# A decoder on one core: LayerNorm statistics of the first two layers by summing passes of ScalarE, and the first group of the first layer placed in front of the tables

## The chip, the cores and the metric

The kernel runs on one core of a Trainium2 chip. The metric is the device time of one execution in microseconds (us), and of several runs the median. A core has five engines that work side by side, each on its own queue, in order: TensorE (PE in the profile; PEld is its weight load), VectorE (DVE), ScalarE (ACT), GpSimd (POOL) and SyncE (SP), which here only issues DMA transfers. An engine that needs another's result waits on a semaphore; everything queued behind the waiting instruction waits too.

## The reference

The input is x, 64 sequences of 128 rows by 256 columns in float32, with a context of the same shape and a mask. Six sublayers follow one another, each of the form x = x + f(layernorm(x)):

```python
def _layernorm(x, axis=-1, eps=1e-05):
    m = jnp.mean(x, axis=axis, keepdims=True)
    v = jnp.var(x, axis=axis, keepdims=True)
    return (x - m) / jnp.sqrt(v + eps)

# 1 window attention: each row attends to 7 neighbours, 16 heads of 16
scores = jnp.einsum('bhld,bhlwd->bhlw', Q, Kw) / sqrt(DH)
fw = softmax(scores) * conn                # conn: a small MLP of the offset
fw = fw / (fw.sum(axis=-1, keepdims=True) + 1e-09)
out = jnp.einsum('bhlw,bhlwd->bhld', fw, Vw) @ wo.T + bo
# 2 first cross attention: queries layernorm(x), keys and values ctx, masked
score = jnp.where(sm == 0, -1e9, q @ k / sqrt(DK))
out = ((softmax(score) * sm) @ v @ Wp.T + bp) * mask
# 3 a slot layer   4 self attention with a bias from distances
# 5 a second cross attention   6 an MLP with quantised values and a convolution
```

The connection table conn depends on weights alone: two layers with a Gelu, and a softmax over the 7 offsets.

## The kernel before, in words

The 64 sequences are worked in 16 groups of four (`GB = 4`). A group's x is one tile of 128 rows by 4 by 256, and eight such tiles are in use in turn. `Flow.reach` (L81) issues the load of a group's x on SP, and the store of finished groups; between the layers x goes through memory in the device. The code lists the operations in a loop order; a scheduler then gives each engine its own order from its estimates, so an engine's queue may differ from the order of the lines.

**Statistics.** There are two ways to get a group's mean and variance. `ln_stats` (L142 to L145) has VectorE make `bn_stats` and `bn_aggr` for each of the four sequences, adds epsilon, and has GpSimd raise the result to -0.5; `row_bias` (L290) then makes -mean × rs on VectorE. `act_means` (L153) and `act_deviations` (L164 to L172) use ScalarE: four Identity passes whose output is thrown away and whose sum is the negative mean, four Square passes with that mean as bias, then one VectorE product-and-sum (L169), the power on GpSimd (L170) and one VectorE product (L172). In the kernel before, the window layer and the first cross layer use the first way; a later layer uses the second.

**The start.** `setup` makes the unit matrix. `prep_window` loads the projection weights, then makes `gather` and `spread` (constant matrices which sum over, or copy to, the 16 columns of a head) and the connection table, in its own PSUM pool `psP`. Only then `stage_window` begins.

**The window layer** (`stage_window`) is a software pipeline over slots, one slot per sequence: `window_project` is a generator whose parts are called one by one, first statistics, then the scaled rows (L299, ScalarE) with the addition of bo into x (L314, GpSimd), transposes (L322, copies L325), and the projections (L194) of q and k per half, copied out by ScalarE (qt L331, pad L336), and of v (pad L341). In step with it run the products q × shifted k on GpSimd (L348, two per sequence), their sums per head on TensorE (L360), once per group the softmax over 7 offsets on VectorE (L376 to L389, exp on ScalarE L379), the spreading of its weights on TensorE (L400), the products with shifted v and their sums on VectorE (L406, L410), and the output projection (L203) whose result VectorE adds to x (L420). At the last slot of the first groups the preparation of the later layers is emitted (`later`): tables and weights for the first cross layer, the slots, the MLP, the self attention and its bias.

PSUM is split into `psA` with three tiles (projections, outputs), `s1A` with one (scores of a group), `scA` with two (spread weights).

**The first cross layer** (`stage_cross0`, about 555 to 1290 us together with the slots): `prep(bi)` is called for each sequence ahead of its attention. At the first sequence of a group it issues the loads of the next group, takes the statistics, scales them by 0.25 (L711) and makes the row bias; then ScalarE writes the normalised query (qp, L720), TensorE transposes it, ScalarE copies it out (qt, L737). Scores are made in two bursts of sixteen heads (L519, tiles sm and se), a maximum on VectorE (L546) and an exp on ScalarE (L542) follow. One tile set of scores exists at a time (`scB`, one buffer).

All SBUF pools wait tile by tile when a new pool takes the memory of an old one (`reuse_waits="tile"`); the PSUM pools wait for the whole old pool.

Of the kernel before, what the change touches and what calls it, by code (L numbers as in the profile page):

```python
# [10 lines left out]
F = mybir.dt.float32  # L11
BF = mybir.dt.bfloat16
AF = mybir.ActivationFunctionType
ALU = mybir.AluOpType
AX = mybir.AxisListType

D = 256
H = 16
DH = 16
S = 128  # L20
WIN = 7
SLOTS = 64
GB = 4
# [88 lines left out]
def load_row(k, pool, name, parts=128):  # L112
    ap = k.a[name]
    t = pool.tile([parts, ap.shape[0]], F, name="t_" + name)
    k.nc.gpsimd.dma_start(out=t, in_=ap.partition_broadcast(parts))
    return t


def psum(k):
    return k.ps.tile([128, 512], F, tag="ps", name="ps")  # L120
# [88 lines left out]
def prep_window(k, pool):  # L209
    nc, a = k.nc, k.a  # L210
    w = Ctx()
    w.wq = load(k, pool, "a_wq")
    w.wk = load(k, pool, "a_wk")
    w.wv = load(k, pool, "a_wv")
    w.wo = load(k, pool, "a_wo")
    w.bo = load_row(k, pool, "a_bo")

    w.gather = pool.tile([128, GB, GB, 8], F, name="gather")
    nc.gpsimd.memset(w.gather, 0.0)
    for b in range(GB):  # L220
        nc.vector.tensor_reduce(
            w.gather[:, b, b, :], k.ident.rearrange("p (h d) -> p h d", d=DH), AX.X, ALU.add
        )

    w.spread = pool.tile([128, GB, 128], F, name="spread")
    for b in range(GB):
        four = pool.tile([128, 4, GB * 8], F, name="four", tag="four", bufs=1)
        nc.vector.tensor_copy(
            four, w.gather[:, b].rearrange("p b h -> p (b h)").unsqueeze(1).to_broadcast([128, 4, GB * 8])
        )  # L230
        p = psum(k)
        nc.tensor.transpose(p[:, 0:128], four.rearrange("p q i -> p (q i)"), k.ident)
        nc.scalar.copy(w.spread[:, b, :], p[:, 0:128])
    w.conn = pool.tile([128, WIN], F, name="conn")
    n = WIN * H
    with k.tc.tile_pool(name="connw", bufs=1) as cp:
        cw1 = load(k, cp, "a_cw1")
        cb1 = load(k, cp, "a_cb1")
        cw2 = load(k, cp, "a_cw2")
        cb2 = load(k, cp, "a_cb2")  # L240
        cw3 = load(k, cp, "a_cw3")
        cb3 = load(k, cp, "a_cb3")
        pos = load(k, cp, "a_pos")
        h1 = cp.tile([n, 32], F, name="h1")
        nc.vector.scalar_tensor_tensor(h1, cw1, pos[:, 0:1], cb1, ALU.mult, ALU.add)
        nc.scalar.activation(h1, h1, AF.Gelu)
        pr = cp.tile([n, 32, 32], F, name="pr")
        nc.vector.tensor_tensor(
            pr, cw2.rearrange("p (j i) -> p j i", i=32),
            h1.unsqueeze(1).to_broadcast([n, 32, 32]), ALU.mult,  # L250
        )
        h2 = cp.tile([n, 32], F, name="h2")
        nc.vector.tensor_reduce(h2, pr, AX.X, ALU.add)
        nc.vector.tensor_tensor(h2, h2, cb2, ALU.add)
        nc.scalar.activation(h2, h2, AF.Gelu)
        nc.vector.tensor_tensor(h2, h2, cw3, ALU.mult)
        cw = cp.tile([n, 1], F, name="cw")
        nc.vector.tensor_reduce(cw, h2, AX.X, ALU.add)
        nc.vector.tensor_tensor(cw, cw, cb3, ALU.add)
        dg = cp.tile([128, n], F, name="dg")  # L260
        nc.gpsimd.memset(dg, 0.0)
        nc.vector.tensor_scalar(dg[:n], k.ident[:n, :n], cw[:, 0:1], None, ALU.mult)
        p = psum(k)
        nc.tensor.matmul(p[:, 0:n], k.ones, dg, start=True, stop=True)
        e = cp.tile([S, WIN, H], F, name="ce")
        pv = p[:, 0:n].rearrange("p (w h) -> p w h", h=H)
        m = cp.tile([S, H], F, name="cm")
        nc.vector.tensor_reduce(m, pv.rearrange("p w h -> p h w"), AX.X, ALU.max)
        nc.vector.tensor_tensor(e, pv, m.unsqueeze(1).to_broadcast([S, WIN, H]), ALU.subtract)
        nc.scalar.activation(e, e, AF.Exp)  # L270
        sm = cp.tile([S, H], F, name="csm")
        nc.vector.tensor_reduce(sm, e.rearrange("p w h -> p h w"), AX.X, ALU.add)
        nc.vector.reciprocal(sm, sm)
        nc.vector.tensor_tensor(
            e, e, sm.unsqueeze(1).to_broadcast([S, WIN, H]), ALU.mult,
        )

        mine = cp.tile([128, H], F, name="mine")
        iv = k.ident.rearrange("p (t c b h) -> p c h t b", t=2, c=2, b=GB)
        for c in range(2):  # L280
            nc.vector.tensor_reduce(mine[:, 8 * c : 8 * c + 8], iv[:, c], AX.XY, ALU.add)
        nc.vector.tensor_tensor(e, e, mine.unsqueeze(1).to_broadcast([S, WIN, H]), ALU.mult)
        nc.vector.tensor_reduce(w.conn, e, AX.X, ALU.add)
    return w


def row_bias(k, pool, mv, rs):
# [16 lines left out]
def window_project(k, w, g, wp, w1, kt, vt):  # L304

    nc = k.nc
    t = Ctx()
    t.g, t.kt, t.vt = g, kt, vt
    k.flow.reach(g + 1)
    mv, rs = ln_stats(k, wp, g)  # L310
    yield t
    xn = w1.tile([S, GB, D], F, tag="xn", name="xn")
    scaled_rows(k, wp, g, mv, rs, xn)
    nc.gpsimd.tensor_tensor(  # L314
        k.x[g], k.x[g], w.bo.unsqueeze(1).to_broadcast([S, GB, D]), ALU.add
    )
    yield t
    xnT = w1.tile([128, 2, GB * S], F, tag="xnT", name="xnT")
    for kc in range(2):
        p = psum(k)  # L320
        for b in range(GB):
            nc.tensor.transpose(  # L322
                p[:, b * S : (b + 1) * S], xn[:, b, kc * 128 : (kc + 1) * 128], k.ident
            )
        nc.scalar.copy(xnT[:, kc, :], p)  # L325
    yield t
    t.qt = wp.tile([128, 2, GB, S], F, tag="qt", name="qt")
    for c in range(2):
        p = psum(k)
        project(k, p, w.wq, c * 128, 128, xnT, 0, GB * S)  # L330
        nc.scalar.activation(  # L331
            t.qt[:, c], p.rearrange("p (b l) -> p b l", l=S), AF.Copy, scale=0.25
        )
        p = psum(k)
        project(k, p, w.wk, c * 128, 128, xnT, 0, GB * S)
        nc.scalar.copy(kt[:, c, :, 3 : 3 + S], p.rearrange("p (b l) -> p b l", l=S))  # L336
        yield t
    for c in range(2):
        p = psum(k)
        project(k, p, w.wv, c * 128, 128, xnT, 0, GB * S)  # L340
        nc.scalar.copy(vt[:, c, :, 3 : 3 + S], p.rearrange("p (b l) -> p b l", l=S))  # L341
    yield t
# [77 lines left out]
    k.nc.vector.tensor_tensor(xb, py[:, 0:D], xb, ALU.add)  # L420


def stage_window(k, w, later):


    nc = k.nc
    with k.tc.tile_pool(name="wa", bufs=2) as wp, k.tc.tile_pool(name="wa1", bufs=1) as w1:
# [8 lines left out]
        def project_part(g):  # L436
            if g in parts:
                groups[g] = next(parts[g], groups.get(g))

        for n in range(-3, GB * (k.G + 3) + 3):  # L440
# [6 lines left out]
            v, vb = divmod(n - 2 * GB - 2, GB)  # L447
            if 0 <= v < k.G:
                values[vb] = window_values(k, w, groups[v], vb, wp)
            if b in (1, 2):  # L450
                project_part(s + 1)
            if b == 0 and s - 2 in groups and s - 2 < k.G:
                window_softmax(k, w, groups[s - 2], wp, w1)
            c, cb = s - 1, b
# [232 lines left out]
def stage_cross0(k, w, slots):  # L687
# [3 lines left out]
    with k.pool("wb", 2) as wp, k.pool("wb1", 1) as w1, k.pool("wb3", 3) as w3:  # L691
# [8 lines left out]
        k.flow.reach(0)  # L700
        stats = {}

        def prep(bi):
            g, b = divmod(bi, GB)
            if b == 0:
                k.flow.reach(min(g + 1, k.G - 1))
                if g + 1 < k.G:
                    cxs[g + 1] = load_group(k, wp, g + 1, 3)
                mv, rs = ln_stats(k, early, g)
                r4 = early.tile([S, GB], F, tag="r4", name="r4")  # L710
                nc.vector.tensor_scalar(r4, rs, 0.25, None, ALU.mult)  # L711
                stats[g] = r4, row_bias(k, early, mv, r4)
            r4, nm = stats[g]
            mk = w.mask[:, bi : bi + 1]
            if b == GB - 1 and g + 1 < k.G:
# [882 lines left out]
def decoder(tc, a):  # L1598
# [8 lines left out]
    k.pool = pool  # L1607

    def scores(name, bufs):
        return tc.tile_pool(name=name, bufs=bufs, space=bass.MemoryType.PSUM)  # L1610

    with ExitStack() as ctx:
        k.res = ctx.enter_context(tc.tile_pool(name="res", bufs=1))
# [12 lines left out]
        w0 = right.enter_context(k.pool("w0", 1, "right"))  # L1626
        with tc.tile_pool(name="wB", bufs=1) as wB, tc.tile_pool(name="wbe", bufs=2) as wbe:
            with tc.tile_pool(name="wA", bufs=1) as wA:
                with scores("psP", 4) as k.ps:
                    wa = prep_window(k, wA)  # L1630

                def prep_b():
                    p.b = prep_cross0(k, wB, wbe)

                def prep_c():
                    p.c = prep_slots(k, w0)

                def prep_d():
                    p.d = prep_proj(k, w1, "d")

                fire = prep_fire(k, w1)

                def prep_bias():
                    next(fire)

                def prep_f():
                    p.f = prep_bitnet(k, k.res)

                with scores("psA", 3) as k.ps, scores("s1A", 1) as k.s1, \
                        scores("scA", 2) as k.sc:  # L1650
                    stage_window(k, wa, [prep_b, prep_c, prep_f, prep_d] + [prep_bias] * 6)
            k.ps = ctx.enter_context(scores("ps", 4))
            score = ExitStack()
            k.sc = score.enter_context(scores("scB", 1))
# [135 lines left out]
```

## Time and profile before

| what | value |
|---|---|
| runs | 3015.18, 3021.71, 3022.23 us; median 3021.71 |
| profiled execution | 3018.02 us, span 3016.2 us |
| mean granted TensorE clock | 0.947 |
| PE busy | 2744.6 us (91%) |
| DVE busy | 2272.4 us (75%) |
| ACT busy | 1676.4 us (56%) |
| POOL busy | 453.7 us (15%) |
| L142 bn_stats, whole kernel | 256 of 402 ns |
| L164 Square pass with sum, later layer | 64 of 493 ns |
| L153 Identity pass with sum, later layer | 64 of 413 ns |
| L348 product on GpSimd | 128 of 2014 ns |

In the profile a group of instructions is a row: line, engine, operation, output and inputs by the program's names, shapes, count, then busy time and mean duration, then the idle time of the engine just before them and what ended it. A row of waits names the engine and the tile that waited, what it waited for, the total in us, the number of times and the longest. A row of the chain is a start, a length and the piece of work that set the end.

The softmax of a window group begins with its maximum (L376). Over the 16 groups that starts at 63.4, 91.6, 127.6, 163.7, 212.9, 239.8, 265.7, 292.6, 331.8, 365.7, 392.7, 419.0, 452.1, 478.0, 503.3 and 527.7 us.

### The profile page before, as it was taken

The numbers are of one execution on the slowest core, as the hardware profiler recorded it, in microseconds if no ns is written. First come the engines' busy times: TensorE is split into PE (matmuls) and PEld (weight loads), VectorE is DVE, ScalarE is ACT, GpSimd is POOL, SyncE is SP. The second block draws the span as 40 slices with busy tenths as digits, with TensorE's granted clock in tenths as the row PEclk, the third lists the DMA queues.
The fourth block names the chain that finished last, engine by engine and source line by source line (L and its number), as shares of the span: only waits on it lengthen the run. The fifth ranks groups of instructions, "written<-read, shape, count | busy, mean of one in ns | idle before, by whom it ended". The sixth has DMA issues, their size and how long they took to land.

```text
span 3016.2 us, 63840 instructions
## 1 busy us (share of the span) xinstructions
PE 2744.6 (91%) x26972; PEld 1769.6 (59%) x26972; DVE 2272.4 (75%) x4341; ACT 1676.4 (56%) x2988; POOL 453.7 (15%) x356
## 2 busy tenths in 40 slices
PE   5789999888988889999999999999999998999998
PEld 2334533576666666666666667666666666444454
DVE  5888789757777777688899889854555545799987
ACT  3132221265666666665666666555556564777764
POOL 7566565000000000100000000110000000000000
PEclk9889899689999999999999999999999899999999
DMA  5101011211111110000200000111111101001100
GB/s 153 42 30 42 29 42 42 70 29 41 58 35 53 44 51 23 29 29 29 78 29 30 30 30 29 36 44 43 43 44 43 43 23 36 26 31 42 36 22 28
DMA packets 60012, 123.83 MB, mean 41 GB/s; under 512 B 9088, under 2 KB 34064, under 8 KB 59472
## 3 DMA queue, kind: packets, MB, share of 16 engines
q1 hardware_dynamic: 59168, 118.28, 11.5%
q8 instruction: 213, 3.49, 0.5%
q0 software_dynamic: 560, 1.49, 0.2%
q14 instruction: 71, 0.58, 0.1%
HBM read 77.76 MB, written 41.98 MB: 40 GB/s over the span
## 4 chain that ended last, share of the span: by engine, by line
PE 52%; DVE 29%; ACT 12%; POOL 3%; DMA 3%; issue 2%; SPq 0%; POOLq 0%; DVEq 0%; ACTq 0%
PE ps L194 9%; PE ps L203 9%; PE sm L519 8%; PE se L519 4%; PE ps L572 4%; PE cv L1442 4%; PE ps L1240 4%; DVE negmax L546 3%; DVE pv L406 2%; DVE sb L533 2%; ACT e L542 2%; DVE e L539 2%; DVE hs L1496 2%; DVE oT L410 2%; PE ps L584 2%
## 5 line engine op out<-in xcount | busy, mean ns | idle before, releaser
L519 PE MATMUL sm<-kt,qt 32*128 32x128 f32 x6144 | 538.3, 298 | 52.5 <-DVE negmax L546 31.2
L519 PEld LDWEIGHTS sm<-kt,qt 32*128 32x128 f32 x6144 | 436.7, 193 | 224.4 <-DVE negmax L546 69.1
L546 DVE TENSOR_REDUCE negmax<-sm 128x8 f32<-128x1024 f32 x256 | 312.3, 1220 | 291.3 <-PE se L519 252.2
L519 PE MATMUL se<-q,kt 32*128 32x128 f32 x6144 | 486.6, 292 | 43.2 <-ACT e L542 25.8
L519 PEld LDWEIGHTS se<-q,kt 32*128 32x128 f32 x6144 | 406.5, 193 | 70.9 <-ACT e L542 31.5
L542 ACT ACTIVATE e<-se 128x1024 f32<-128x1024 f32 x256 | 261.3, 1021 | 181.6 <-PE se L519 177.0
L348 POOL TENSOR_TENSOR pr<-pad,qt 128x896 f32<-128x896 f32 x128 | 254.8, 2014 | 137.0 <-PE s L360 97.7
L577 ACT COPY avs<-ps 128x512 f32<-128x512 f32 x192 | 112.0, 583 | 150.5 <-PE ps L572 150.5
L533 DVE TENSOR_TENSOR sb<-sm,bias_s 128x1024 f32<-128x1024 f32 x128 | 156.1, 1220 | 46.9 <-PE se L519 35.8
L145 POOL TENSOR_TENSOR ln_rs<-ln_ve,expo 128x4 f32<-128x4 f32 x64 | 66.2, 1036 | 734.6 <-DVE ln_ve L144 624.6
L540 ACT ACTIVATE e<-e 128x1024 f32<-128x1024 f32 x128 | 135.2, 1056 | 71.7 <-DVE e L539 70.9
L406 DVE TENSOR_TENSOR pv<-sc,pad 128x896 f32<-128x896 f32 x128 | 138.9, 1091 | 25.9 <-PE sc L400 25.8
L539 DVE TENSOR_TENSOR e<-se,bias_t 128x1024 f32<-128x1024 f32 x128 | 155.3, 1214 | 0.0
L546 DVE TENSOR_REDUCE negmax<-sb 128x8 f32<-128x1024 f32 x128 | 154.6, 1208 | 0.0
L572 PE MATMUL ps<-e,dva 128*32 128x128 f32 x4096 | 149.0, 289 | 2.7 <-ACT e L542 2.0
L410 DVE TENSOR_REDUCE oT<-pv 128x128 f32<-128x896 f32 x128 | 138.9, 1091 | 1.0
L572 PEld LDWEIGHTS ps<-e,dva 128*32 128x32 f32 x4096 | 111.4, 115 | 44.4 <-issue 30.5
L400 PE MATMUL sc<-fw,spread 32*128 32x448 f32 x512 | 106.5, 663 | 32.7 <-DVE pv L406 27.8
L560 DVE TENSOR_TENSOR q<-ps,qt 128x512 f32<-128x512 f32 x192 | 130.6, 680 | 1.7 <-PE ps L558 1.7
L584 PE MATMUL ps<-ident,avs 128*128 128x128 f32 x768 | 120.8, 282 | 0.1
L142 DVE BATCH_NORM_STATS2 ln_st<-x 128x6 f32<-128x256 f32 x256 | 98.1, 402 | 23.4 <-DMA x<-ef 14.7
L170 POOL TENSOR_TENSOR as_r<-as_s,expo 128x4 f32<-128x4 f32 x16 | 16.1, 1008 | 552.9 <-DVE as_s L169 552.9
(360 smaller groups left out, 5913.4 us busy)
## 6 DMA issues: line engine op xcount, KB each, us to landing
x<-in_x_dram SPq DMA_DIRECT2D x16, 512.0 KB
kt<-in_ctxT_dram SPq DMA_DIRECT2D x128, 64.0 KB
ab<-x SPq DMA_DIRECT2D x16, 512.0 KB
x<-ab SPq DMA_DIRECT2D x16, 512.0 KB
cx<-in_ctx_dram SPq DMA_DIRECT2D x16, 512.0 KB
cd<-x SPq DMA_DIRECT2D x16, 512.0 KB
x<-cd SPq DMA_DIRECT2D x16, 512.0 KB
de<-x SPq DMA_DIRECT2D x16, 512.0 KB
```

The costliest lines, as they stand in the source:

```text
L194: k.nc.tensor.matmul(out, w[:, kc, c0 : c0 + cn], rhsT[:, kc, n0 : n0 + n], start=(kc == 0), stop=(kc == 1),)
L203: k.nc.tensor.matmul(out, aT[:, kc, :], w[:, kc, :], start=(kc == 0), stop=(kc == 1))
L348: k.nc.gpsimd.tensor_tensor(pr[:, c], shift_windows(t.kt, b, c), t.qt[:, c, b, :].unsqueeze(1).to_broadcast([128, WIN, S]), ALU.mult,)
L406: nc.vector.tensor_tensor(pv, bc[th][:, :, 0 : WIN * 64].rearrange("p c (l w) -> p c l w", w=WIN), shift_windows2(t.vt, b, th), ALU.mult,)
L410: nc.vector.tensor_reduce(oT[:, :, 64 * th : 64 * th + 64], pv, AX.X, ALU.add)
L519: k.nc.tensor.matmul(ts[side][:, rr, c * S : (c + 1) * S], st[rows, c, :], mv[rows, c, :], start=True, stop=True,)
L533: nc.vector.tensor_tensor(sb, src, bias_s[:, hf * 2 : hf * 2 + 2, :], ALU.add)
L539: nc.vector.tensor_tensor(e, est, bias_t[:, hf * 2 : hf * 2 + 2, :], ALU.add)
L542: nc.scalar.activation(e, est, AF.Exp)
L546: nc.vector.tensor_reduce(b.lay.extra(b.nm, hf * 2), src.rearrange("p r (c m) -> p r c m", m=S), AX.X, ALU.max, negate=True,)
L572: nc.tensor.matmul(av[32 * r : 32 * r + 32, c * S : (c + 1) * S], b.va[:, b.lay.head(c, r), :], b.e[r // 2][:, r % 2, c * S : (c + 1) * S] ...
L584: nc.tensor.transpose(tv[:, c * S : (c + 1) * S], b.avs[:, c, :], k.ident)
```

## The change

Four parts.

1. In the window layer a group's statistics are taken by `act_means` and `act_deviations`, as two parts of the generator, and the tile `xn` of the normalised rows takes their thrown-away output. The generator of the next group is now advanced in three slots of four (`b >= 1`), where it was two.
2. `prep_window` only loads weights. `prep_spread` and `prep_connection` are called inside the slot loop, at n = 4 and n = 6, so that the first group's projection is emitted in front of them. `prep_spread` uses one PSUM tile and one copy for all four matrices, and borrows the tile `xnT`. The pool `psP` is gone.
3. PSUM pools, too, wait tile by tile.
4. In the first cross layer the statistics of group g + 1 are taken by passes of ScalarE during group g (at its third sequence), those of group 0 before the loop. The passes write to one junk tile. Both results are scaled by 0.25.

```diff
@@ prep_window: the tables become functions of their own
+    return w
+
+def prep_spread(k, w, pool, w1):
     w.gather = pool.tile([128, GB, GB, 8], F, name="gather")
...
+    xnT = w1.tile([128, 2, GB * S], F, tag="xnT", name="four")
+    four = xnT[:, 0].rearrange("p (b q i) -> p b q i", b=GB, q=4)
+    p = psum(k)
     for b in range(GB):
-        four = pool.tile([128, 4, GB * 8], F, name="four", tag="four", bufs=1)
         nc.vector.tensor_copy(
-            four, w.gather[:, b].rearrange(...).to_broadcast([128, 4, GB * 8])
-        )
-        p = psum(k)
-        nc.tensor.transpose(p[:, 0:128], four.rearrange("p q i -> p (q i)"), k.ident)
-        nc.scalar.copy(w.spread[:, b, :], p[:, 0:128])
+            four[:, b], w.gather[:, b].rearrange(...).to_broadcast([128, 4, GB * 8])
+        )
+        nc.tensor.transpose(
+            p[:, b * 128 : (b + 1) * 128], four[:, b].rearrange("p q i -> p (q i)"), k.ident
+        )
+    nc.scalar.copy(w.spread, p.rearrange("p (b i) -> p b i", b=GB))
+
+def prep_connection(k, w, pool):
     w.conn = pool.tile([128, WIN], F, name="conn")
@@ window_project
-    mv, rs = ln_stats(k, wp, g)
+    xn = w1.tile([S, GB, D], F, tag="xn", name="xn")
+    means = act_means(k, wp, g, xn)
     yield t
-    xn = w1.tile([S, GB, D], F, tag="xn", name="xn")
-    scaled_rows(k, wp, g, mv, rs, xn)
+    rs, add = act_deviations(k, wp, g, xn, means)
+    yield t
+    scaled_rows(k, wp, g, None, rs, xn, add)
@@ stage_window
-            if b in (1, 2):
+            if b >= 1:
                 project_part(s + 1)
+            if n == 4:
+                prep_spread(k, w, pool, w1)
+            if n == 6:
+                prep_connection(k, w, pool)
@@ stage_cross0
+        def statistics(g):
+            junk = early.tile([S, D], F, tag="junk", name="junk", bufs=1)
+            rs, add = act_deviations(
+                k, early, g, junk.unsqueeze(1).to_broadcast([S, GB, D]),
+                act_means(k, early, g, junk.unsqueeze(1).to_broadcast([S, GB, D])),
+            )
+            r4 = early.tile([S, 2, GB], F, tag="r4", name="r4")
+            nc.vector.tensor_scalar(r4[:, 0], rs, 0.25, None, ALU.mult)
+            nc.vector.tensor_scalar(r4[:, 1], add, 0.25, None, ALU.mult)
+            stats[g] = r4[:, 0], r4[:, 1]
+
+        statistics(0)
+
         def prep(bi):
...
-                mv, rs = ln_stats(k, early, g)
-                r4 = early.tile([S, GB], F, tag="r4", name="r4")
-                nc.vector.tensor_scalar(r4, rs, 0.25, None, ALU.mult)
-                stats[g] = r4, row_bias(k, early, mv, r4)
+            if b == 2 and g + 1 < k.G:
+                statistics(g + 1)
@@ decoder
     def scores(name, bufs):
-        return tc.tile_pool(name=name, bufs=bufs, space=bass.MemoryType.PSUM)
+        return tc.tile_pool(
+            name=name, bufs=bufs, space=bass.MemoryType.PSUM, reuse_waits="tile"
+        )
...
-                with scores("psP", 4) as k.ps:
-                    wa = prep_window(k, wA)
+                wa = prep_window(k, wA)
```

The three lines of code that call these functions at the start and pass the pool on are left out.

More of the change, by code (lines that the diff above doesn't have):

```diff
@@ L216, in prep_window @@
     w.bo = load_row(k, pool, "a_bo")
+    return w
+def prep_spread(k, w, pool, w1):
+    nc = k.nc
     w.gather = pool.tile([128, GB, GB, 8], F, name="gather")
@@ L225, in prep_window @@
     w.spread = pool.tile([128, GB, 128], F, name="spread")
+    xnT = w1.tile([128, 2, GB * S], F, tag="xnT", name="four")
+    four = xnT[:, 0].rearrange("p (b q i) -> p b q i", b=GB, q=4)
+    p = psum(k)
     for b in range(GB):
-        four = pool.tile([128, 4, GB * 8], F, name="four", tag="four", bufs=1)
         nc.vector.tensor_copy(
-            four, w.gather[:, b].rearrange("p b h -> p (b h)").unsqueeze(1).to_broadcast([128, 4, GB * 8])
+            four[:, b], w.gather[:, b].rearrange("p b h -> p (b h)").unsqueeze(1).to_broadcast([128, 4, GB * 8])
         )
-        p = psum(k)
-        nc.tensor.transpose(p[:, 0:128], four.rearrange("p q i -> p (q i)"), k.ident)
-        nc.scalar.copy(w.spread[:, b, :], p[:, 0:128])
+        nc.tensor.transpose(
[3 more added lines that the diff above has]
+def prep_connection(k, w, pool):
+    nc = k.nc
     w.conn = pool.tile([128, WIN], F, name="conn")
@@ L283, in prep_window @@
         nc.vector.tensor_reduce(w.conn, e, AX.X, ALU.add)
-    return w
 def row_bias(k, pool, mv, rs):
@@ L420, in window_out, with stage_window @@
     k.nc.vector.tensor_tensor(xb, py[:, 0:D], xb, ALU.add)
-def stage_window(k, w, later):
+def stage_window(k, w, pool, later):
     nc = k.nc
@@ L1650, in decoder @@
                         scores("scA", 2) as k.sc:
-                    stage_window(k, wa, [prep_b, prep_c, prep_f, prep_d] + [prep_bias] * 6)
+                    stage_window(k, wa, wA, [prep_b, prep_c, prep_f, prep_d] + [prep_bias] * 6)
             k.ps = ctx.enter_context(scores("ps", 4))
```

## The prediction

> **What bounds the kernel now.** I read the totals, then the chain that ended last, then the three stretches that the change touches: the start (0 to 63 us), the window layer (63 to about 540), the first cross layer (600 to 1240).
>
> ```profile
> PE 2744.6 (91%) x26972; PEld 1769.6 (59%) x26972; DVE 2272.4 (75%) x4341; ACT 1676.4 (56%) x2988; POOL 453.7 (15%) x356
> ...
> PE 52%; DVE 29%; ACT 12%; POOL 3%; DMA 3%; issue 2%; SPq 0%; POOLq 0%; DVEq 0%; ACTq 0%
> ```
>
> TensorE leads, so only the places where something else makes it wait can pay. The start is one. Pieces of its chain (start us, length us, what ran or was waited for), then the busy time of 39.4 to 57.8 us by engine:
>
> ```profile
> 12.02 9.06 DMA t_mask<-in_mask_dram
> ...
> 23.25 0.75 DVE ln_st L142 x2
> ...
> 37.42 7.14 POOL pr L348 x4
> ...
> 57.83 5.63 DVE ln_nm L290
> 63.45 0.55 DVE m L376
> ```
> ```profile
> 39.40:57.80 18.40, 18.40 (x72) 7.13 (x71) 0.00 (x0) 7.18 (x13) 18.40 (x11) 1.00 0.58 200
> ```
>
> VectorE reaches the first group's statistics at 23.25, behind the tables and a mask's DMA, although x of that group landed at about 4.2 us. The first GpSimd product starts at 37.42 and the first softmax at 63.45; for 18.4 us between, VectorE does nothing.
>
> In the window layer I took single groups (columns: PE, PEld, DVE, ACT, POOL busy us, granted clock, DMA share, GB/s), then the waits of 60 to 540 us (total, times, longest), then groups of instructions:
>
> ```profile
> 239.80:265.70 25.90, 24.51 (x114) 10.64 (x113) 24.46 (x39) 7.06 (x13) 19.04 (x11) 1.00 0.09 34
> 292.60:365.70 73.10, 73.10 (x482) 41.41 (x481) 53.78 (x94) 14.22 (x26) 37.68 (x23) 0.84 0.08 27
> ...
> 478.00:503.30 25.30, 23.91 (x114) 10.37 (x113) 23.18 (x39) 5.09 (x9) 16.38 (x10) 1.00 0.12 42
> 600.00:1240.00 640.00, 570.78 (x7339) 430.63 (x7334) 456.52 (x1218) 400.64 (x707) 27.51 (x38) 0.95 0.13 42
> ```
> ```profile
> POOL pr L348 <- PE s L360: 97.7, 24, 14.3
> ...
> PE sc L400 <- DVE pv L406: 27.6, 24, 4.1
> ```
> ```profile
> L142 DVE BATCH_NORM_STATS2 ln_st<-x 128x6 f32<-128x256 f32 x66 | 24.9, 402 | 2.3 <-DMA x<-ab 1.2 <-DMA x<-in_x_dram 1.1
> L290 DVE SCALAR_TENSOR_TENSOR ln_nm<-ln_mv,ln_rs 128x4 f32<-128x4 f32 x12 | 19.4, 1614 | 25.1 <-POOL ln_rs L145 25.1
> ```
>
> A quiet group takes 25.9 us with PE at 24.5 and DVE at 24.5: two engines that lock step by step, with ScalarE at 7. From 292.6 to 365.7 PE is busy throughout at a clock of 0.84: nothing done for VectorE pays there.
>
> **The change, part by part.**
>
> *Start.* First group's statistics: four Identity passes, four Square passes on ScalarE. The trace has both in a later layer: 0.41 us at a pitch of 0.40, and 0.49. With the 0.85 us between the two sets seen there: 4×0.40 + 4×0.49 + 0.85 = 4.4, from 4.3 to 8.7 us. Then VectorE 0.16, GpSimd's power 1.02, VectorE 0.16 (rows L169, L170, L172): 10.1. Four scaled rows at 0.52: 12.2. From the first xn to the first projection was 3.28 us (27.15 to 30.43), so projections start at 13.4 at the earliest, last 6.30 and end in a 0.60 copy: 20.3. GpSimd's queue has the second group's power ahead of the first product; that group's passes come on ScalarE behind the xnT copies (about 13.4), plus 4.4, plus a qt copy of 0.60, VectorE 0.16 and power 1.02: 19.6 to 20.5. So the first product starts at about 20.5 instead of 37.4: 17 us.
>
> From first product to first softmax it was 26.0 us; eight products at 1.9, one addition of bo at 2.35 and about 1.5 of scores are the least, 19. So the softmax comes at 40 to 47, for 63.45: 16 to 23 earlier. Against it: what was in front now lies beside. VectorE's tables are short (product and sum of the connection net 1.22 each, a dozen steps of 0.2 to 0.3) and fill its idle stretch; on ScalarE two Gelu and one exp with table loads of 1.28 come among the copies. SP is reordered: x1 to x3 ahead of the seven table loads, and the load of maskr now waits until the connection's scratch memory is free. VectorE's mask product (225 ns once its DMA is there) stands ahead of the second group's L169, so the power and GpSimd's first product wait for the mask's landing: by 17 us if only b_wp is in front of it, 21 as before, 25 at worst; the last costs 4. Likewise the first softmax's `ec` stands behind the scaling of maskr, whose load is only issued after the tables: 0 to 9 us (a landing cost t_mask 9.06 in a full queue), I take 2, nearer to an idle queue. From 63 to 240 us VectorE is 157.7 of 176.4 busy, so an early start is passed on, unless weights are late (one wait on t_g_w is 4.84 at 105). I book **-15**, with -7 and -22 as ends.
>
> *Window statistics, groups 1 to 15.* VectorE loses 4 × (0.39 pitch) = 1.6 us, the row bias (0.15 free, 1.9 where a GpSimd product holds it up) and gains two of 0.16. [...] But GpSimd's list now reads power, addition of bo (which waits for the scaled rows, hence for L172), products: GpSimd is idle when L172 runs, so I take 0.16. [...]
>
> What this is worth: the last full group (478 to 503) has DVE 1.3 lower and PE 0.6 lower than a quiet one and is 0.6 shorter, so a quiet group follows PE, and I book 0.4 for each of nine: -4 (0 to -12). The early groups, 28 to 49 us long because preparation fills VectorE, gain 1.6 to 3.5 each; the two in the throttled stretch nothing; five at 2: -10 (-4 to -16). ScalarE's 4.4 us lie in its 18.8 idle us.
>
> New serial chain, booked at 0: last products (2 × 1.89), power 1.1, L172 0.16, scaled row 0.55, qt copy 0.60, with handovers about 7.6 us, while PE has 7.9 to 8.4 of other work between the same points. If that cover goes, PE stalls for what is over: 0 to 2 a group.
>
> *First cross layer.* Out: 1.6 VectorE us a group and the power between statistics and qp. In: two products of 0.16 and 8 passes. They share one junk tile, so each waits for the one before: about 0.6 (0.41 and the 0.19 accumulator read), 4.9 in all, in ScalarE's 15 idle of 40 us. Part of the passes stands between a query row and an exp, and behind that exp waits the next score burst, since the score tile is single:
>
> ```profile
> ACT e L542 <- PE se L519: 95.9, 40, 4.8
> ```
>
> ScalarE already waits 2.4 us on average for those scores, which covers most of the 1.6 to 3.7 us of passes. VectorE's 1.6 was partly idle time. I take 0 (-15 to +20).
>
> *PSUM pools.* Waiting by tile lets a new pool start before the old one has drained, at two borders; no row shows this alone: 0 to -3, I take -1.
>
> Sum: -15 -4 -10 +0 -1 = **-30**. On the profiled execution (3018.0 us, span 3016.2, 1.8 outside) this is 2988. It lies 3.7 below the median of 3021.7; against the median the sum gives 2992. I take **2990**.
>
> **The rivals.**
>
> 1. *The start's gain is lost again.* Weights of later layers are loaded in the same order; if groups 0 to 3 are paced by DMA, the 15 shrink to 5: 3000. For it: t_g_w, and the maskr load that SP now holds for the tables. Against: the DMA share after 63 us is 0.11.
> 2. *The window chain is longer than its cover.* With 1 us lost in 15 groups the window gains go: 3005. For it: a slack below 1 us. Against: PE can be ahead of it by its three buffers.
> 3. *Slower: exps behind passes.* In the cross layer up to four Identity (2.4) and four Square (2.7) stand ahead of one exp. If PE has the scores ready earlier than 2.4 us, up to 3.7 us a group delay exp and the next burst: 16 × 3.7 = 59, 3021.7 - 31 + 59 = 3049. It decides from (31 + 9)/16 = 2.5 us a group, when the kernel is slower. For it: one score tile, ScalarE on the chain for 12%. Against: the 95.9 us of waits.
> 4. *It does nothing*: if the window layer follows PE alone and the start is bought back by the throttled clock (0.84) coming earlier: 3018.
>
> **How the numbers follow.** Forecast 0.56, rival 1 0.14, rival 2 0.12, rival 3 0.10, rival 4 0.08. The ends of the parts (start 8 either way, window 12 upward, 14 downward with fw, cross 15 to 20) put forecast and rivals 1 and 2 between 2967 and 3014. Of 0.18 for rivals 3 and 4 half of rival 4 lies inside 3016, so 2967 to 3016 keeps 8 in 10. No change is 0.3%, 9 us, about what a measurement of this kernel can tell. Faster: 0.55 + 0.13 + 0.09 = 0.77; within: 0.01 + 0.01 + 0.03 + 0.06 = 0.11; slower: the rest of rivals 3 and 4, 0.12.
>
> **What would show it.** Start: first product at 20 to 22 us, first softmax's maximum at 40 to 48. Window: quiet groups of 25.3 to 25.6 with DVE near 22.5; L172 at 0.16, not 1.6; no new wait of the projections on the qt copy. Cross: groups of 41 us as before, exp's wait for scores down by about the passes' length while TensorE's wait for exp stays. Wrong, if a maskr or mask wait of several us stands on VectorE before 60 us, if PE waits for scaled rows in each group, or if the cross stretch grows.

## The result, and the profile after

The changed kernel is slower: 3034.71 us (median of 9 runs, 3026.62 to 3038.62) against 3018.28 us of the kernel before (median of 9, 3009.8 to 3026.59). The ratio is 1.0055, 95% interval 1.0039 to 1.0071. Forecast were 2990 us, in a range of 2967 to 3016. The profiled execution of the changed kernel took 3038.62 us, span 3036.9; the two profiles differ by 20.6 us, the medians by 16.4.

The changed kernel's totals, and its chain by engine, from the page:

```profile
PE 2758.4 (91%) x26946; PEld 1778.2 (59%) x26972; DVE 2220.7 (73%) x4101; ACT 1794.7 (59%) x3497; POOL 455.3 (15%) x356
...
PE 50%; DVE 27%; ACT 13%; DMA 3%; POOL 3%; issue 2%; SPq 0%; POOLq 0%; DVEq 0%; ACTq 0%
```

VectorE lost 52 us and ScalarE gained 118, as the change says. TensorE, whose instructions are the same, is busy 14 us longer. That is the first hint: the same matmuls ran at a lower granted clock (0.942 for 0.947).

Where the time went is read from four marks: the start of the first window softmax, of the sixth, of the eleventh and of the sixteenth (row L376 before, L392 after), and from the maxima of the cross layers (L546, L566). Times in us:

| mark | before | after | difference |
|---|---|---|---|
| first softmax | 63.4 | 45.6 | -17.8 |
| sixth | 239.8 | 216.3 | -23.5 |
| eleventh | 392.7 | 377.9 | -14.8 |
| sixteenth | 527.7 | 527.3 | -0.4 |
| first maximum of the cross layer | 564.7 | 562.8 | -1.9 |
| its 61st sequence | 1199.0 | 1216.6 | +17.6 |
| last maximum of the second cross layer | 2553.8 | 2574.2 | +20.4 |

So the start came as forecast, ten window groups gave all of it away, and the first cross layer lost nearly 20 us. After it little happens (2.8 us).

**Start.** Some pieces of the chain of the changed kernel (start, length, what):

```profile
29.05 1.90 DVE dg L277
...
40.97 1.03 POOL as_r L170
42.02 1.92 DVE as_a L172
...
45.55 1.68 DMA t_maskr<-in_maskr_dram
47.25 1.99 DVE t_maskr L815
```

The first scaled row starts at 10.1 us, the first GpSimd product at 21.0, the softmax at 45.6. The table work now lies between GpSimd's products, and VectorE's part of it waits: 1.90 us for dg and 1.98 for the scaling of maskr, which took 0.28 and 0.41 in the kernel before, with no GpSimd instruction beside them.

Of the 17.8 us, 3.7 are no merit of the change. In the kernel before, the row bias in front of the first softmax (L290, the piece at 57.83 in the prediction) took 5.63 us, because three GpSimd products ran one after another beside it. In experiments 6 and 10, which leave VectorE's and GpSimd's work up to there as it was, it met one product, took 1.9 us, and the softmax began at 59.1 and 59.3.

**Window groups.** Two of the groups of the changed kernel (length; PE, PEld, DVE, ACT, POOL busy; granted clock; DMA share; GB/s):

```profile
216.30:247.00 30.70, 27.18 (x114) 11.58 (x113) 24.58 (x32) 10.50 (x29) 21.39 (x12) 0.89 0.14 48
438.70:469.30 30.60, 26.93 (x114) 11.38 (x113) 24.35 (x34) 14.51 (x45) 20.03 (x12) 0.89 0.09 35
```

A quiet group takes 30.6 us where it took 25.9. TensorE has the same 114 matmuls and is busy 2.4 us longer, at a clock of 0.89 instead of 1.00. In all fourteen traces the stretches at half clock begin on a fixed grid of 3.413 us and last whole steps of it (the last of a trace is cut by its end). Four steps of this grid in the second of these groups:

```profile
445.29:448.70 3.41, 1.02 (x4) 0.30 (x4) 3.41 (x7) 3.41 (x16) 1.89 (x1) 1.00 0.00 0
448.70:452.12 3.42, 2.51 (x8) 0.70 (x12) 3.42 (x6) 0.59 (x4) 0.00 (x0) 0.50 0.00 0
452.12:455.53 3.41, 3.41 (x13) 1.85 (x6) 3.18 (x6) 0.00 (x0) 2.56 (x2) 0.50 0.00 0
455.53:458.94 3.41, 3.41 (x12) 1.33 (x14) 2.35 (x5) 0.60 (x1) 3.21 (x3) 1.00 0.00 0
```

TensorE waits 2.4 us from 445.1 on and is busy for 1.02 us of the first step. With the next step its clock is halved, for 6.8 us; a second gap, of 1.1 us, falls into this time. In the window layer of the fourteen traces (45 to 540 us), half clock followed on all 89 steps at full clock in which TensorE was busy for less than 40%, on 104 of 173 with 40 to 70%, on 9 of 68 with 70 to 80%, and on none of 114 with 80 to 95%. Waiting is not the only cause: it also followed on 28 of 1102 steps busy for 95% or more, two in each kernel, as at 298.5 us in the kernel before. Why is open.

What makes TensorE wait stands in the chain of the next group, which repeats it:

```profile
463.44 2.60 DMA ab<-x
466.05 3.23 DMA x<-ab
469.31 0.52 ACT junk L153 x2
...
472.70 0.47 ACT pad L357
473.18 0.50 ACT junk L164 x2
473.68 0.47 ACT e L395
...
474.17 1.81 DVE ec L397
```

`junk` is the cross layer's: its first groups' statistics are ready to be scheduled as soon as x has been stored by the window layer (ab<-x) and loaded again (x<-ab), and they stand in ScalarE's queue in front of the window softmax's exp (L395). ScalarE waits for the reload, then makes passes; the softmax is late, the spreading of its weights (L416) is late, TensorE stands, its clock drops. And the store of the next group waits for that: the loop closes. The row of the waits from 377 to 540 us:

```profile
ACT junk L153 <- DMA x<-ab: 41.3, 6, 22.1
```

In the kernel before, VectorE did the same statistics in the same stretch, and waited 1.2 us for the reload in all. Only a part of the 41.3 us costs time: from 438.7 to 500 us the reload has 5.3% of the chain, 3.2 us.

The group at 216.3 has no such passes, and the same gap. There `ec` took 2.09 us (at 219.4) instead of 0.62, and a GpSimd product was running beside it. The kernel before has one such group too, at 419.0 (its row of `ec`, then its window):

```profile
L381 DVE TENSOR_TENSOR ec<-e,conn x1: 2311/2311/2311, 423.4 to 423.4; 128x448 f32<-128x448 f32 x1
```
```profile
419.00:452.10 33.10, 27.72 (x114) 11.67 (x113) 27.49 (x41) 7.05 (x13) 19.06 (x11) 0.85 0.13 48
```

**First cross layer.** A piece of the chain in the changed kernel:

```profile
838.46 0.70 DVE rz L1013
...
839.19 0.63 ACT rz L1014
839.82 0.41 ACT junk L153 x2
...
841.33 0.60 ACT junk L164 x2
841.93 0.32 ACT nn L1021
...
847.81 1.00 POOL as_r L170
...
849.23 1.02 POOL ln_rs L145
...
850.46 1.09 ACT c_xn L313 x2
851.56 0.91 ACT e L562
```

The passes stand between two steps of the slot layer (rz, nn), whose other steps stand in front of the next maximum on VectorE; later GpSimd's power for the passes (as_r) stands ahead of the slot layer's (ln_rs), and its scaled rows (c_xn) ahead of an exp. The passes have become part of the chain: L153 has 2.3% and L164 2.2% of it from 600 to 1240 us. In the same stretch an exp waits less for its scores, 83.2 us for the 95.9 of the kernel before, since the passes now fill part of that time:

```profile
ACT e L562 <- PE se L539: 83.2, 36, 4.2
```

### The profile page after: what moved, and what is told of

It reads as the page before. It is cut to its first block, busy times and chain, and to the rows that moved or that the text cites. A ratio compares the mean times of both kernels' runs of the same rounds, so it can differ in the third digit from the quotient of the medians.

```text
span 3036.9 us, 64050 instructions
## 1 busy us (share of the span) xinstructions
PE 2758.4 (91%) x26946; PEld 1778.2 (59%) x26972; DVE 2220.7 (73%) x4101; ACT 1794.7 (59%) x3497; POOL 455.3 (15%) x356
## 4 chain that ended last, share of the span: by engine, by line
PE 50%; DVE 27%; ACT 13%; DMA 3%; POOL 3%; issue 2%; SPq 0%; POOLq 0%; DVEq 0%; ACTq 0%
PE ps L203 9%; PE ps L194 8%; PE sm L539 8%; PE se L539 4%; PE ps L592 4%; PE ps L1271 3%; DVE negmax L566 3%; PE cv L1473 3%; DVE hs L1527 2%; ACT e L562 2%; PE sc L416 2%; DVE sb L553 2%; DVE e L559 2%; PE ps L604 2%; DVE pv L422 2%
## 5 line engine op out<-in xcount | busy, mean ns | idle before, releaser
L566 DVE TENSOR_REDUCE negmax<-sm 128x8 f32<-128x1024 f32 x256 | 312.4, 1220 | 295.2 <-PE se L539 254.3
L170 POOL TENSOR_TENSOR as_r<-as_s,expo 128x4 f32<-128x4 f32 x48 | 48.7, 1014 | 719.0 <-DVE as_s L169 618.3
L566 DVE TENSOR_REDUCE negmax<-sb 128x8 f32<-128x1024 f32 x128 | 154.7, 1209 | 0.0
L416 PE MATMUL sc<-fw,spread 32*128 32x448 f32 x512 | 104.8, 675 | 38.1 <-DVE pv L422 31.1
L145 POOL TENSOR_TENSOR ln_rs<-ln_ve,expo 128x4 f32<-128x4 f32 x32 | 32.3, 1010 | 606.9 <-DVE ln_ve L144 578.3
L313 ACT ACTIVATE xn<-x,as_a,as_r 128x256 f32<-128x256 f32 x128 | 68.4, 592 | 59.2 <-DVE as_a L172 59.2
```

The lines of the kernel that those rows point to most:

```text
L416: nc.tensor.matmul(bc[th][:, c, 0 : WIN * 64], w.spread[32 * q : 32 * q + 32, b, :], t.fw[32 * q : 32 * q + 32].rearrange("p l w -> p (l w ...
L566: nc.vector.tensor_reduce(b.lay.extra(b.nm, hf * 2), src.rearrange("p r (c m) -> p r c m", m=S), AX.X, ALU.max, negate=True,)
```

## The experiments

Theory A: the cross layer's passes on ScalarE cost twice, in the window layer's queue and in their own. Rival B: the window layer's own new chain stretches its groups. Three runs after that separate engine from place in the cross layer (C, D, H, I), two test how a late softmax turns into time (F, G). Marks, each row from one profiled execution (us):

| kernel | first softmax | 11th | 16th | cross layer, first | 61st sequence |
|---|---|---|---|---|---|
| before | 63.4 | 392.7 | 527.7 | 564.7 | 1199.0 |
| after | 45.6 | 377.9 | 527.3 | 562.8 | 1216.6 |
| without the cross part | 46.9 | 376.9 | 512.8 | 549.8 | 1183.6 |
| cross part alone | 63.6 | 396.2 | 547.4 | 583.1 | 1238.9 |
| passes after the window | 47.0 | 374.7 | 517.7 | 558.9 | 1218.6 |
| window part alone | 59.8 | 385.9 | 521.7 | 558.7 | 1196.1 |
| start alone | 59.2 | 391.2 | 525.6 | 562.6 | 1196.2 |

**1. The change without its cross part.**

```diff
-        def statistics(g): ...          # passes of ScalarE, a group ahead
-            if b == 2 and g + 1 < k.G:
-                statistics(g + 1)
+                mv, rs = ln_stats(k, early, g)      # at b == 0, as before
```

> The change without its fourth part: the first cross layer takes its statistics by VectorE as before. Theory A (passes of the cross layer stand in ScalarE's queue inside the window layer, in front of the window's exp, and later in front of the cross layer's exp): the window groups from the eleventh on take 26 to 27 us instead of 30.5, the cross layer is as before, so the start's lead of some 15 us stays: about 3003 us, 15 below before. Rival B (the window layer's own new chain of power, scaled row and qt copy stretches the groups): they stay at 30, only the cross layer's 18 us come back: about 3017 us.

Measured: 3003.66 us, ratio to before 0.9955 (0.9937 to 0.9972). Theory A's number. From the eleventh to the sixteenth softmax it is 135.9 us (before 135.0, after 149.4), and the cross layer is as before. But not all of its groups are short; two that follow each other:

```profile
433.40:458.70 25.30, 23.97 (x114) 10.44 (x113) 23.34 (x41) 10.62 (x29) 18.02 (x11) 1.00 0.11 39
458.70:488.40 29.70, 26.40 (x114) 11.25 (x113) 25.33 (x38) 5.09 (x9) 18.06 (x11) 0.89 0.11 39
```

With `ec` at 0.61 and the sum `se` (L402, se<-se,scn) at 0.21 the group takes 25.3 us, 0.6 less than before; with 1.35 and 1.44 it takes 29.7 at the lower clock. So B names a real cost, though not by its chain.

**2. The cross part alone.**

```diff
+        def statistics(g): ...          # into the kernel before, nothing else
```

> The kernel before with the fourth part alone (cross statistics by ScalarE, a group ahead). Theory A: window groups from the eleventh on go from 26 to about 30 (four or five groups, 15 to 20 us), the cross layer loses another 18: about 3051 us. Rival B: the window layer is untouched, only the cross layer loses: about 3036 us.

3056.11 us, ratio 1.0122 (1.0101 to 1.0144). The window groups from the eleventh softmax on take 151.2 us for 135.0, although that layer's code is untouched, and from the first cross maximum to the 61st sequence it is 655.8 for 634.3. Theory A, with both halves.

**3. Passes kept out of the window layer.**

```diff
-            junk = early.tile([S, D], F, tag="junk", name="junk", bufs=1)
+            junk = w1.tile([S, D], F, tag="junk", name="junk", bufs=1)
```

> The whole change, but the cross layer's junk tile lies in memory that the window layer still uses, so that no cross pass can run before the window layer is over. Theory A: the late window groups go back to 26 to 27 us and gain some 15; the passes of the first groups crowd at the border and cost up to 5 there; the cross layer's own loss of 18 stays: about 3020 to 3025 us. Rival B: late window groups stay at 30: 3035 us or more.

3038.50 us, ratio 1.0064 (1.0044 to 1.0085). A's number fails. The stretch from the eleventh to the sixteenth softmax falls to 143.0 us, less than half of the way back; four of its five groups still take 28 to 30, by collisions as in experiment 1. At the border it is 4 us more than before, and 10 more over the first eight sequences, since eight groups' passes now crowd there. Putting the passes elsewhere only moves the cost.

**4. Window statistics alone.**

```diff
-    mv, rs = ln_stats(k, wp, g)
+    means = act_means(k, wp, g, xn)
     yield t
-    scaled_rows(k, wp, g, mv, rs, xn)
+    rs, add = act_deviations(k, wp, g, xn, means)
+    yield t
+    scaled_rows(k, wp, g, None, rs, xn, add)
```

> The kernel before with the window layer's statistics by ScalarE alone (first part). Theory A: a quiet group stays at 25.5 to 26, the first softmax near 63 us, the whole about 3010 to 3018 us. Rival B: quiet groups at about 30, the whole 3040 us or more.

3013.85 us, ratio 0.9986 (0.9973 to 0.9999): a gain of 4 to 5 us that is just clear of noise, and neither theory's groups: some are 25.2, some 30.3, as in experiment 1.

**5. The start alone.**

```diff
-                with scores("psP", 4) as k.ps:
-                    wa = prep_window(k, wA)
+                wa = prep_window(k, wA)         # tables at n == 4 and n == 6
```

> The kernel before with the second part alone: first group's projection in front of the tables, statistics still by VectorE, PSUM pools as before. If the parts add up (the change without its cross part gave -15, the window statistics alone -5), the rest is some -10: about 3008 us, with the first softmax near 48. If the start's gain needs the statistics on ScalarE, because VectorE is held by masks and tables, it is 3014 or more.

3011.64 us, ratio 0.9990 (0.9978 to 1.0001). In its profile VectorE takes x of the first group at 4.8 us, but its scaled rows start only at 18.2 and the first product at 29.6 (21.0 in the changed kernel), since the row bias (L304) stands in VectorE's queue behind the statistics of the next groups, which wait until x of these lands (the last at 16.2); the power was done at 8.6. The first softmax comes only at 59.2, behind the tables and more statistics on VectorE. So most of the start's gain needs both parts: -4 (with an interval that reaches 0) and -5 alone, -15 with each other.

**6. PSUM pools alone.**

```diff
-        return tc.tile_pool(name=name, bufs=bufs, space=bass.MemoryType.PSUM)
+        return tc.tile_pool(
+            name=name, bufs=bufs, space=bass.MemoryType.PSUM, reuse_waits="tile"
+        )
```

> The kernel before with the third part alone (PSUM pools wait tile by tile). Both theories: 0 to -3 us, 3016 to 3019.

3020.98 us, ratio 1.0016 (1.0003 to 1.0029). From the sixteenth softmax to the first cross maximum it is 37.0 us in both: nothing is gained at that border. The first softmax comes 4 us earlier, because L290 met one product and not three, and a gap of 5.9 us follows; from the second softmax to the fourth the clock is 0.91 and 0.81, in the kernel before 0.95 and 0.86.

**7. Cross statistics a group ahead, but by VectorE.**

```diff
-            rs, add = act_deviations(k, early, g, junk..., act_means(k, early, g, junk...))
+            mv, rs = ln_stats(k, early, g)
```

> The whole change, but the cross layer's statistics, still a group ahead and at the third sequence, are taken by VectorE. Theory C (what costs in the cross layer is ScalarE's passes in front of an exp): the cross layer is as before, about 3003 us. Rival D (the place costs: a group ahead, its power stands in GpSimd's queue in front of the slot layer's power): the cross layer keeps more than half of its 18 us: 3013 us or more.

3003.72 us, ratio 0.9951 (0.9934 to 0.9969). Theory C: with the place kept and the engine restored the loss is gone, in both layers.

**8. By ScalarE, in the group itself.**

```diff
-        statistics(0)
-            if b == 2 and g + 1 < k.G:
-                statistics(g + 1)
+                statistics(g)                   # at b == 0
```

> The whole change, but the cross layer's statistics by ScalarE are taken at the first sequence of the group itself instead of a group ahead. Theory C: the passes are still in front of exps, in the window layer and in the cross layer: 3030 to 3040 us. Rival D: with the place restored the cross layer's loss goes: about 3017 us.

3035.02 us, ratio 1.0058 (1.0042 to 1.0074). With the engine kept and the place restored the loss stays, in both layers (148.8 us from the eleventh to the sixteenth softmax). D falls.

**9. Half of the passes.**

```diff
-            rs, add = act_deviations(...)       # four Square passes
+            nc.vector.tensor_scalar(ss, nm, 0.0, 1.0, ALU.mult, ALU.add)
```

> The whole change, but the cross layer makes only the four Identity passes and leaves the four Square passes out (its variance is taken as 1). Everything else of the new chain stays: ScalarE, VectorE's two steps, GpSimd's power, a group ahead. Theory H (the length of the passes on ScalarE counts): about half of the cross layer's loss goes: 585 to 590 us from the 9th to the 61st sequence fall to about 579, before being 570; the late window groups keep the wait for the reload and stay near 30: about 3023 to 3027 us. Rival I (the order of the chain counts, not the length): the stretch stays at 585 or more, 3033 us or more.

3026.90 us, ratio 1.0038 (1.0024 to 1.0051). From the 9th to the 61st sequence it is 579.2 us: before 570.3, after 587.8. That is half of the loss, as theory H has it: in the cross layer the length of the passes on ScalarE is what counts. In the window layer nothing comes back (150.2 us from the eleventh to the sixteenth softmax), but not only for the reload that H names. The steps behind the passes count there as well: in the twelfth group two of them stand in VectorE's queue in front of `ec`, and both meet a GpSimd product:

```profile
413.35 1.03 POOL as_r L729
414.40 1.92 DVE as_a L731
...
416.40 1.84 DVE r L734
418.24 0.53 DVE ec L397
```

**10. A longer softmax in the kernel before.**

```diff
+    nc.vector.tensor_tensor(ec, e, w.conn..., ALU.mult)     # twice more
```

> The kernel before with the window softmax's product ec made three times over (same result, 1.25 us of VectorE added to each group between the exp and fw). Theory F (what costs is a stretch of about 3 us in which TensorE waits within a group: its granted clock is halved afterwards for some 6.6 us, worth 3 us): the quiet groups go from 25.9 to about 30 with a clock near 0.89, more than three times what was added. Rival (the clock does not depend on the wait): they go to 27.2 at the most, with a clock of 1.00 or 0.94.

3042.60 us, ratio 1.0085 (1.0064 to 1.0105). The gap in a quiet group grows from 1.1 to 1.9 us only. Two such groups:

```profile
240.00:269.40 29.40, 27.22 (x114) 11.53 (x113) 26.82 (x42) 7.06 (x13) 19.83 (x11) 0.88 0.14 49
269.40:297.10 27.70, 25.52 (x114) 11.29 (x113) 26.22 (x42) 7.06 (x13) 19.76 (x11) 0.94 0.10 32
```

Both have the same gap of 1.9 us; one had 6.8 us at half clock, the other 3.4. Neither expectation holds as written: two of the five quiet groups come near 30, three to 27.7. The dip follows the wait, but its length is not settled by it. In the sixth, seventh and tenth to fourteenth groups of all fourteen traces:

| gaps of TensorE in the group | groups | no half clock | 3.4 us | 6.8 us | 10.2 us |
|---|---|---|---|---|---|
| 0.5 us | 9 | 9 | | | |
| 1.1 us | 29 | 13 | 14 | 2 | |
| two of 0.6 us | 4 | 4 | | | |
| 1.8 to 1.9 us | 5 | | 3 | 2 | |
| 2.5 to 3.2 us | 20 | | 9 | 11 | |
| 3.3 us and more | 31 | | 1 | 27 | 3 |

An estimate from this table, if half of the time at half clock is lost: a gap of 1.1 us costs another 1.1 us on average, and gaps of 2.5 to 3.2 us another 2.6.

**11. Without the addition of bo.**

```diff
-    nc.gpsimd.tensor_tensor(
-        k.x[g], k.x[g], w.bo.unsqueeze(1).to_broadcast([S, GB, D]), ALU.add
-    )
```

> The change without its cross part, and without the addition of bo to x by GpSimd (the output lacks bo). Theory F with GpSimd as the cause of the late softmax: 2.35 us less on GpSimd per group, its products are over before ec and the sum se, which take 0.62 and 0.21 in the quiet groups; the groups of 30 go to 25 to 26, the whole to 2985 to 2992 us. Rival G (the chain of power, scaled rows and qt copy holds TensorE up): the groups of 30 stay, 3000 us or more.

2992.03 us, ratio 0.9919 (0.9904 to 0.9934): 12 us below experiment 1. From the tenth softmax on `ec` takes 0.61 to 0.63 and `se` 0.21 to 0.34, and the five groups from 373 us on take 132.0 us in place of 135.9; they are 24.4 to 28.5 us long, not 25 to 26, since a gap of 1.1 us alone brought half clock in three of them. The sixth and seventh group still have `se` at 1.5 and take 28 to 30. F's number holds to its edge, with 3 us of it from the cross layer, which F does not explain; its mechanism holds in part: GpSimd's products, pushed back by the addition, are what the softmax runs into, but not in every group.

**12. Without cross part and without PSUM part.**

```diff
-            name=name, bufs=bufs, space=bass.MemoryType.PSUM, reuse_waits="tile"
+            name=name, bufs=bufs, space=bass.MemoryType.PSUM
```

> The change without its cross part and without the PSUM part. If tile by tile waits cost, as the run of that part alone has it (about 3 to 5 us): 2999 to 3001 us. If that was chance: 3004.

3001.85 us, ratio 0.9950 (0.9935 to 0.9964), against 3003.66 of experiment 1: the difference is within the spread of both. The PSUM part is worth nothing that these runs can tell. With those of experiments 1 and 7 this is the fastest version with the full result, and all three beat both kernels.

## Why the prediction was wrong

*Start, booked -15: right.* First scaled row 10.1 us as worked out, first product 21.0 for 20.5, softmax 45.6 within 40 to 47. Both waits that were named came, the mask's at 19.5 us and maskr's at 47.25, and cost no more than booked. A part was luck: the 26.0 us that the prediction read from first product to first softmax hold 3.7 us of L290 standing through two more products than in other kernels.

*L172 at 0.16: right in the steady groups*, 1.9 twice in the start, where a product runs beside it, and 1.25 once, at 487 us. A hold-up by GpSimd was weighed for L172, and missed where it struck: at `ec` (2.09 us for 0.62 at 219.4) and the sum `se` (1.46 for 0.21 at 251.8), two VectorE instructions of the same softmax. GpSimd's products moved onto them when the power and the addition of bo moved behind the last products. The prediction listed the new order and asked only who waits for it, not what now runs beside it.

*`fw` under the moved addition, in the ends of the range:* no run shows this term. In the changed kernel the addition of bo ran beside `fw` in no group; `fw` took 1.61 and 1.83 us in two groups, beside products, and 0.60 to 0.63 in the other fourteen. In the kernel before it had taken 1.60 to 1.93 in six.

*Early groups, booked -10:* from the first to the sixth softmax -5.7 (-7.7 without the cross part). With the start it is -23.5 at the sixth softmax for the -25 booked, so the sum was nearly right and its division off.

*Quiet groups, booked -4: the first of two steps that failed.* "A quiet group follows PE" is right for a group without collision (25.2 to 25.3 for 25.9, -0.6 for the -0.4 booked). But the step took TensorE's 24.5 us as given, and put the new chain at nothing. They are 24.5 us at full clock, and two gaps of 3.5 us in all cost 2.4 more afterwards. The sum valued a wait of TensorE at its length; the runs put it at about twice that. The ten groups from the sixth softmax on took 294.0 to 297.3 us in the four kernels with this part and no cross passes (experiments 1, 4, 7 and 12). With the window code of before they took 287.9 us in the kernel before and 292.2 and 293.0 in experiments 5 and 6. So this part lost 1 to 9 us there instead of gaining 4.

*"ScalarE's 4.4 us lie in its 18.8 idle us": the other step that failed, and the dearer one.* With the cross layer booked at 0 it is the whole of the fourth part, and that part turned a gain into a loss: 31 us, from 3003.66 to 3034.71. In the late window groups there were not 4.4 but 9 us of passes: those of the cross layer stand in the same queue. The trace of before showed VectorE making the cross layer's statistics from 395 us on, inside the window layer; their move to ScalarE had to be counted there, with the wait for the reload of x, in front of the exp. Experiment 2 puts this at 16 us in the window layer, the difference of the changed kernel and experiment 1 at 13.5.

*First cross layer, booked 0 with +20 as its end:* +19.5. Rival 3 named the mechanism, exps behind passes; ten groups made their passes within the layer at a cost of some 2 us each, below its ceiling of 3.7. The cover that the prediction counted on, ScalarE's wait for scores, fell only from 96 to 83 us: of some 44 us of passes from 600 us on (nine groups at 4.9), 13 lay in it.

*PSUM, booked -1:* nothing to be told.

Rival 2 had the right place and the wrong chain. Rival 1 fell: at the sixth softmax the lead had grown, so the weight loads took nothing of it. The DMA that held up the late window groups, the reload of x for the cross layer, stood in no rival. Of the forecast of -30, -15 is what the change gives when its fourth part is left out.

## What to carry to other kernels

When work moves to an engine with idle time, look in the new order for everything that lands in that queue, of the next stage too, and for what stands right behind it: idle time in total is no cover for an exp that another engine waits for. In a kernel like this one, price a wait of TensorE of 1 us or more at about twice its length, since a stretch of 3.4 or 6.8 us at half clock can follow (an estimate from the table of experiment 10). And when GpSimd's work shifts in time, list all VectorE instructions that it will now run beside and could hold up: here `ec` (2.09 us for 0.62), the sum `se` (1.46 for 0.21), `fw` (1.93 for 0.60), the row bias (1.9 for 0.15), L169 and L172 (up to 3.56 and 1.92 for 0.16), the scaling of maskr (1.98 for 0.41), the product dg (1.90 for 0.28) and the copy c_bin (L876 before, L907 after; 1.18 for 0.29).

## What the runs showed of the hardware that was not expected

- TensorE's clock was halved after steps of a 3.413 us grid in which it was busy for up to 80%, so also without a gap as long as a step. With the same gap of 1.9 us the time at half clock was 3.4 us in one group and 6.8 in another; with one of 1.1 us it was 0, 3.4 or 6.8.
- The product `ec` took 0.59 to 0.63 us in the window layers of all fourteen traces whenever no GpSimd instruction ran beside it (154 times), and up to 2.38 when one did. The 4-element row bias took 0.15 alone, 1.9 beside one product and 5.63 beside three: the end of the first did not free it.
- Steps outside the softmax were held as well: the scaling of maskr took 1.98 us for 0.41, the product dg 1.90 for 0.28. Not held were, in the window layers of all fourteen traces, the sum of e (0.62 us at most beside GpSimd), the maximum m (0.62) and the reciprocal (0.55); the product with an input in PSUM (pv) had a median of 1.08 us with GpSimd and without, but took 2.57 and 2.64 once each in the two kernels, beside the iota that fills nd.
